# Graph convolution with experts: two dense chunks become gathered parts, and the counting one-hots are made in batches

## The chip, the cores and the metric

The kernel runs on one core of a Trainium2 chip. The metric is the device time of one execution in microseconds (us). A core has a matrix engine (TensorE, PE in the profile; PEld is its loading of the stationary operand), a vector engine (VectorE, DVE), a scalar engine (ScalarE, ACT), a general engine (GpSimd, POOL), a synchronisation engine (SyncE, SP) and sixteen DMA engines behind queues. A queue is named by the engine that issues to it, and "POOLq" or "ACTq" in a row is that engine's issuing of a transfer.

## The reference

The input is a matrix `x` of 6250 nodes by 256 features, and 200,000 edges (`src`, `dst`), sorted by `dst`. The destinations are drawn as a square of a uniform number, so that low node numbers have many edges and high ones few. The core of what is computed:

```python
deg_out = clip(segment_sum(ones, src, n), 1.0)
deg_in = clip(segment_sum(ones, dst, n), 1.0)
h = feats * rsqrt(deg_out)[:, None]
m = segment_sum(h[src], dst, n) * rsqrt(deg_in)[:, None]
xx = m @ W_gc + b_gc + feats @ W_res + b_res
core = moe_ff(xx, ...)        # top 2 of 64 experts, 256 -> 512 -> 256, gelu
y = xx + core
y = batch_norm(y) * gamma + beta
out = layernorm(feats + y)
```

The line that matters here is `m`: for every node, the sum of the rows `h[src]` over the edges that end in it.

## The kernel before

The nodes stand in 50 tiles (`NT`) of 125 (`TP`), the edges in 1563 parts of 128 (`NGU`): a part is one column of 128 lanes. The program goes through these stages; the times are those of the profiled execution.

**Degrees and projection (0 to 185 us).** For blocks of parts DVE makes one-hot matrices of the source node's tile (`hot_col`) and of its place in the tile (`hot_row`, both in the helper `hot_pairs`, L243), and TensorE multiplies them (L452), which counts the out-degrees. Between these it projects the features (`project`, L408), whose transposed tiles ACT copies (`fT`, L402). The function `split` (L153 to L342) divides each source number into tile and place; it runs for a head of 128 parts first, and for all others in the third iteration (i = 2), followed by `windows()`. In the head, ACT copies `hi_b` (L334) and `col_b` (L335), and DVE goes on from `col_b` (L340). Ahead of these ACT issues transfers of weights on its own queue (L309, L310).

**Transition (185 to 228 us).** The scale of each node is made, the projected rows `hrow` are scaled and written to `h_dram`, and DVE computes `key`, which says for each part of the dense kind and each lane the node's place in the part's window (L538 to L543); parts that don't fit are marked with a large number and go to a fallback loop after the stage, which has nothing to do for these inputs.

**Gather and dense stage (228 to 1095 us).** Two ways of summing share it. `_plan` divides the parts between them ahead of time, in the program that builds the kernel: it adds dense chunks from the first part on, as long as a modelled time of TensorE lies under a number of microseconds for each part that is left to gather.

- *Dense chunks* (the first `GD` = 1025 parts, 31 chunks, where nodes have many edges). A chunk is a run of `n` groups of `k` parts, each group covering a window of `w` nodes. For every part DVE makes a one-hot of the key against `iota_h` (`hot_of`, `hotk`, L628: 50 tiles x w columns for each lane) by a comparison with a scalar. For every eight parts it makes `lo`, the one-hot of the source's place in its tile. TensorE multiplies the two into `pc` (`count`, L638), so that `pc` counts how often each source is summed into each of the w nodes. ACT casts the counts of a group to their place in `counts` (L646); the place comes from a register that it loads from `places`. Then `multiply` (L653, L654) goes through the 50 tiles with two matmuls each, counts times `hrow`, into `sm`; ACT copies the result (`sums`, L664), and `spread` (L670, L672) puts it in its window of nodes and adds the end of the chunk before, with the one-hots `to` and `overd`. `sums_done` copies that (`resd`, L596) and SP's queue writes it to `z_dram` (L599). While chunk c is multiplied, the counts of chunk c + 1 are made.
- *Gathered parts* (the other 538, in 32 windows). POOL issues an indirect DMA that fetches the 128 rows of `h_dram` into one of six row buffers (`fetch`, L580). DVE makes a one-hot of the keys for four parts at a time (`hot`, L803), and two matmuls add the rows into the window (`pg`, L585, L586). A window that is done takes the carry of the one before (L824), is copied (`resg`, L596) and written like the others.

Beside these, finished pairs of node tiles are turned into `x` (L688 to L723), and routed to experts.

The order is written out by hand: the generator `dense()` yields pieces of work with a modelled time each, and the loop after it places one `gather(n)` whenever the modelled time passes `LEAD + n * every`, where `every` spreads the gathers evenly. In `gather`, the fetch for a buffer follows the matmuls that read it:

```python
add_rows(live["pg"], ring[n % NR], hot, g == g0, top and g == g0 + k - 1)
if n + NR < len(rows):
    fetch(ring[n % NR], srcg[:, ...])
```

**Routing (1095 to 1184 us), experts (1184 to 1655 us), norms (to the end).** Routing makes prefix counts with matmuls against triangular and all-one matrices (`upto_b`, `ones_b`). The experts' tokens are fetched and put back with indirect DMAs, and TensorE multiplies (L1273, L1285).

Of the kernel before, what the change touches and what calls it, by code (L numbers as in the profile page):

```python
# [127 lines left out]
LG = -(-GD // 32) * 32  # L134

# [10 lines left out]
def gnn_moe_kernel(ctx, tc, x_in, src, dst, bases, nexts, firsts, parts, lasts, W_gc, b_gc, W_res, b_res, Wg, bg, w1, b1, w2, b2,  # L146
# [47 lines left out]
    iota_h = const.tile([128, 512], FP16, name="iota_h")  # L194
    for k in range(4):
        V.tensor_scalar(iota_h[:, k * 128:(k + 1) * 128], iota_f, float(k * 128), None, op0=ALU.add)
# [7 lines left out]
    upto_b = const.tile([128, 128], BF16, name="upto_b")  # L204
    V.tensor_scalar(upto_b, iota_f, pidx, -1.0, op0=ALU.is_gt, op1=ALU.add)
    ones = const.tile([128, 128], F32, name="ones")
    V.memset(ones, 1.0)
    ones_b = const.tile([128, 128], BF16, name="ones_b")
    V.memset(ones_b, 1.0)
# [9 lines left out]
    with tc.tile_pool(name="edges", bufs=1) as ep, ExitStack() as later:  # L219
# [4 lines left out]
        key = ep.tile([128, GD], F32, name="key")  # L224
# [28 lines left out]
        with tc.tile_pool(name="deg", bufs=1) as dp, tc.tile_pool(name="hot", bufs=2) as hp, \  # L253
                tc.tile_pool(name="ld", bufs=2) as ld, \
                tc.tile_pool(name="ps_deg", bufs=1, space=PSUM) as ps_deg, \
                tc.tile_pool(name="ps_a", bufs=2, space=PSUM) as ps_a:
            srcf = dp.tile([128, NGR], F32, name="srcf", tag="a")
# [6 lines left out]
            G.dma_start(out=key[:, :GD], in_=bases.to_broadcast([128, GD]))  # L264
# [64 lines left out]
            def split(a, b):  # L329
# [4 lines left out]
                S.activation(hi_b[:, a:b], hi[:, a:b], AF.Copy)  # L334
                S.activation(col_b[:, a:b], hi[:, a:b], AF.Copy, scale=2.0)  # L335
# [92 lines left out]
            for i in range(NGR // CG):  # L428
# [5 lines left out]
                if i == 2:  # L434
                    split(HEAD, NGR)
                    G.tensor_tensor(following[:, :GD], following[:, :GD], key[:, :GD], ALU.subtract)
# [46 lines left out]
            fit, t1 = flags[:, 0, :], flags[:, 1, :]  # L483
            kd = dp.tile([128, GD], FP16, name="kd")
            V.tensor_tensor(kd, dstf[:, :GD], key[:, :GD], ALU.subtract)
# [57 lines left out]
            V.tensor_scalar(key[:, :GD], kd, BIG, None, op0=ALU.subtract)  # L543
# [20 lines left out]
        with tc.tile_pool(name="cnt", bufs=1) as cp, tc.tile_pool(name="rows", bufs=1) as rp, \  # L564
# [6 lines left out]
            NR = 6  # L571
# [44 lines left out]
            KB = 7  # L616
            hots, los, live = {}, {}, {}

            def hot_of(g):

                if g >= GD:
                    return
                if g % PAIRS == 0:
                    los[g // PAIRS] = hc.tile([128, PAIRS // 2, 128, 2], BF16, name="lo")
                    hot_pairs(los[g // PAIRS], lo_b, g, PAIRS, 128)
                w = DENSE[groups[g][0]][2]
                hots[g] = hc.tile([128, NT * w], BF16, name="hotk", bufs=KB, padded_shape=[128, NT * WMAX])
                V.tensor_scalar(hots[g], iota_h[:, :NT * w], key[:, g:g + 1], None, op0=ALU.is_equal)  # L628

            def count(g):  # L630
# [9 lines left out]
                hot_of(g + KB)  # L640
# [119 lines left out]
            def dense():  # L760
# [4 lines left out]

                for g in range(KB):
                    hot_of(g)
# [142 lines left out]

    b1T = ctx.enter_context(tc.tile_pool(name="b1pool", bufs=1)).tile([128, 4, E], F32, name="b1T")
# [20 lines left out]

    iota_e = rt.tile([TP, E, NT], BF16, name="iota_e")
# [587 lines left out]
```

## Time and profile before

| what | value |
| --- | --- |
| median of 3 runs | 1791.05 us (1790.22 to 1792.17) |
| profiled execution, its own time | 1785.81 us |
| its span | 1784.0 us |
| mean TensorE clock granted | 0.926 |
| TensorE busy | 1463.9 us, 82% of the span |
| VectorE busy | 991.2 us, 56% |
| ScalarE busy | 702.0 us, 39% |
| GpSimd busy | 907.8 us, 51% |

The profile is of one execution. A group's row reads: line, engine, operation, output and input names, shapes, count, then busy us and mean ns of one, then the idle time of that engine just before these instructions and what ended most of it. In a timeline row the first number is the start in us, the second the duration in us, and what stands in brackets is the idle time before it and what ended it. A window's row gives a stretch of the span, its length, the busy time of the five engines with their instruction counts, the granted TensorE clock, the DMA engines' busy share and GB/s. A row of waits has total us, times, and the longest in us.

### The profile page before, as it was taken

The numbers are of one execution on the slowest core, as the hardware profiler recorded it, in microseconds if no ns is written. First come the engines' busy times: TensorE is split into PE (matmuls) and PEld (weight loads), VectorE is DVE, ScalarE is ACT, GpSimd is POOL, SyncE is SP. The second block draws the span as 40 slices with busy tenths as digits, with TensorE's granted clock in tenths as the row PEclk, the third lists the DMA queues.
The fourth block names the chain that finished last, engine by engine and source line by source line (L and its number), as shares of the span: only waits on it lengthen the run. The fifth ranks groups of instructions, "written<-read, shape, count | busy, mean of one in ns | idle before, by whom it ended". The sixth has DMA issues, their size and how long they took to land. (4 is left out here: it accounts for less than half of the span.)

```text
span 1784.0 us, 31696 instructions
## 1 busy us (share of the span) xinstructions
PE 1463.9 (82%) x10296; PEld 1213.0 (68%) x10296; DVE 991.2 (56%) x2594; ACT 702.0 (39%) x1707; POOL 907.8 (51%) x984
## 2 busy tenths in 40 slices
PE   3999168899898899989899896369999999999730
PEld 2555047677788888888888895158878887777520
DVE  7999886666666555545454551962222222222787
ACT  2343663333455554445444441032222222222248
POOL 3241436666676666666666664025655666554000
PEclk8999678999999999999999998579999999999875
DMA  5798766776776777677776774917867888675934
GB/s 146 225 276 262 238 180 181 195 199 186 208 215 195 197 216 213 183 211 206 203 207 195 217 205 119 211 48 244 268 207 240 253 245 257 212 244 179 223 87 127
DMA packets 221104, 362.19 MB, mean 203 GB/s; under 512 B 24819, under 2 KB 149613, under 8 KB 220929
## 3 DMA queue, kind: packets, MB, share of 16 engines
q1 hardware_dynamic: 158039, 180.12, 34.7%
q0 software_dynamic: 55328, 172.48, 34.1%
q10 hardware_dynamic: 7562, 7.47, 1.5%
q8 instruction: 84, 1.38, 0.3%
q14 instruction: 91, 0.75, 0.1%
HBM read 279.11 MB, written 74.47 MB: 198 GB/s over the span
## 5 line engine op out<-in xcount | busy, mean ns | idle before, releaser
L580 POOL DMA_INDIRECT r<-h_dram,srcg x538 | 554.7, 1031 | 303.5 <-issue 109.9
L653 PE MATMUL sm<-hrow,counts 125*128 125x258 f32 x1550 | 502.2, 340 | 7.9 <-ACT counts L646 5.4
L646 ACT CAST counts<-pc 128x300 f32 (+7 forms) x804 | 355.9, 443 | 335.4 <-PE pc L638 147.0
L628 DVE TENSOR_SCALAR hotk<-iota_h,key 128x300 bf16<-128x300 f16 (+7 forms) x1025 | 272.5, 305 | 326.1 <-PE pc L638 159.4
L654 PE MATMUL sm<-hrow,counts 125*128 125x256 f32 x1550 | 417.6, 284 | 0.7 <-issue 0.7
L653 PEld LDWEIGHTS sm<-hrow,counts 125*128 125x128 f32 x1550 | 304.4, 196 | 68.8 <-issue 57.0
L638 PE MATMUL pc<-hotk,lo 128*128 128x300 bf16 (+7 forms) x1025 | 282.1, 303 | 82.3 <-issue 35.5
L654 PEld LDWEIGHTS sm<-hrow,counts 125*128 125x128 f32 x1550 | 301.2, 194 | 2.1 <-issue 1.5
L1275 ACT ACTIVATE hT<-ph,b1c 128x128 f32<-128x128 f32 (+8 forms) x256 | 108.6, 437 | 352.0 <-PE ph L1273 219.0
L1285 PE MATMUL py<-w2s,hT 128*128 128x256 f32 (+3 forms) x992 | 240.5, 385 | 3.4 <-issue 1.9
L1273 PE MATMUL ph<-xgT,w1s 128*128 128x128 f32 (+8 forms) x1024 | 211.3, 349 | 8.9 <-issue 5.4
L1273 PEld LDWEIGHTS ph<-xgT,w1s 128*128 128x128 f32 x1024 | 170.5, 192 | 42.7 <-issue 19.7
L1285 PEld LDWEIGHTS py<-w2s,hT 128*128 128x128 f32 (+3 forms) x992 | 166.4, 176 | 44.7 <-issue 6.6
L585 PE MATMUL pg<-r,hot 128*128 128x258 f32 x538 | 178.5, 332 | 19.5 <-issue 11.1
L1239 POOL DMA_INDIRECT y_dram<-ys,dest x124 | 119.1, 961 | 146.4 <-DVE ys L1288 83.5
L1239 POOL DMA_INDIRECT xg<-x_dram,ids x124 | 119.1, 960 | 111.2 <-DVE ids L1191 71.3
L586 PE MATMUL pg<-r,hot 128*128 128x256 f32 x538 | 153.3, 285 | 0.0
L1288 DVE TENSOR_TENSOR ys<-py,b2s 128x256 f32<-128x256 f32 (+3 forms) x124 | 51.3, 420 | 166.9 <-PE py L1285 117.7
L638 PEld LDWEIGHTS <-lo 128*128 128x128 bf16 x1025 | 90.0, 102 | 73.7 <-issue 23.0
L1263 DVE COPY xgT<-pte 128x256 f32<-128x256 f32 (+7 forms) x64 | 38.5, 601 | 182.2 <-PE pte L1261 71.8
L585 PEld LDWEIGHTS pg<-r,hot 128*128 128x128 f32 x538 | 104.8, 195 | 38.9 <-issue 25.0
L586 PEld LDWEIGHTS pg<-r,hot 128*128 128x128 f32 x538 | 104.7, 195 | 0.9
(321 smaller groups left out, 1775.1 us busy)
## 6 DMA issues: line engine op xcount, KB each, us to landing
w1s<-in_L_gnn_w_dram SPq DMA_DIRECT2D x64, 512.0 KB
w2s<-in_L_gnn_w_dram SPq DMA_DIRECT2D x64, 512.0 KB
y_dram<-zeros SPq DMA_DIRECT2D x48, 256.0 KB
yr<-y_dram SPq DMA_DIRECT2D x25, 448.0 KB
r<-h_dram,srcg POOLq DMA_INDIRECT x538
b2s<-in_L_gnn_b_dram SPq DMA_DIRECT2D x64, 128.0 KB
h_dram<-hrow SPq DMA_DIRECT2D x5, 1344.0 KB
z_dram<-zeros ACTq DMA_DIRECT2D x7, 903.0 KB
```

What stands on the lines that cost most here:

```text
L580: G.indirect_dma_start(out=f32(r[:, :2 * D]), out_offset=None, in_=h_dram[:, :], in_offset=bass.IndirectOffsetOnAxis(ap=idx, axis=0))
L585: T.matmul(pg, hot, r[:, D:], start=first, stop=False)
L586: T.matmul(pg[:, :D], hot, r[:, :D], start=False, stop=last)
L628: V.tensor_scalar(hots[g], iota_h[:, :NT * w], key[:, g:g + 1], None, op0=ALU.is_equal)
L638: T.matmul(pc, los[g // PAIRS][:, r // 2, :, r % 2], hots.pop(g), start=(i == 0), stop=(i == k - 1))
L646: S.copy(counts[c % 2][:, :, ds(live["at"][j % 8], w)], pc.rearrange("p (t w) -> p t w", w=w))
L653: T.matmul(sm, by, hrow[:, t, D:], start=(t == 0), stop=False)
L654: T.matmul(sm[:, :D], by, hrow[:, t, :D], start=False, stop=(t == NT - 1))
L1239: w = G.indirect_dma_start(**kw)
L1273: T.matmul(ph[:, :m], w1s[:, kk, c * 128:(c + 1) * 128], xgT[:, kk, :m], start=(kk == 0), stop=(kk == 1))
L1275: S.activation(hT[:, c, :m], ph[:, :m], AF.Gelu, bias=b1_e[:, c:c + 1])
L1285: T.matmul(py[:n], hT[:, c, k * 128:k * 128 + n], w2s[:, c, :], start=(c == 0), stop=(c == 3))
```

## The change

1. The number of microseconds that the plan sets against each gathered part goes from 1.29 to 1.2. Two chunks fewer are dense: 29 chunks with 988 parts in place of 31 with 1025. The other 29 are as before; the widest of their windows is 8 and no longer 9. Gathered are 575 parts in 34 windows in place of 538 in 32. Since the modelled work is less and the gathers more, `every` falls from 1.117 to 0.981 modelled us.
2. The fetches have eight row buffers and no longer six, so that the order holds eight fetches ahead of the first gathered matmul.
3. `resd` and `resg` have one buffer each and no longer two.
4. The one-hots `hotk` are made in batches: one comparison of two tensors for several parts at once (36 columns a tile, so 18 parts for a window of 2, 12 for 3, 8 for 4, 6 for 5 and 6, 4 for 7 and 8), laid out in pairs of parts. There are 189 of these in place of 1025 comparisons with a scalar. Two batches are held in place of seven parts. The `lo` of a block of eight parts is made one block ahead (`lo_of`).
5. The comparison needs `key` as fp16; it is computed in place of `kd`, and the windows' bases have a tile of their own, `base`.
6. In the head of `split`, DVE makes `col_b` and no longer ACT, and ACT makes `hi_b` after it.
7. The constants `ones`, `ones_b` and `upto_b` are made in the pools that use them (degrees, experts, routing), and not at the start for the whole program.

```diff
-    while 16.0 + 1.03 * (pe + (NGU - g) * 0.265) < (NGU - g) * 1.29:
+    while 16.0 + 1.03 * (pe + (NGU - g) * 0.265) < (NGU - g) * 1.2:
...
+LANES = 36
...
-        key = ep.tile([128, GD], F32, name="key")
+        key = ep.tile([128, GD + GD % 2], FP16, name="key")
...
+        cuts, cut_of = [], {}
+        for c, (g0, k, w, n) in enumerate(DENSE):
+            a = g0
+            while a < g0 + k * n:
+                b = min(a - a % 2 + LANES // w // 2 * 2, g0 + k * n)
+                for g in range(a, b):
+                    cut_of[g] = len(cuts)
+                cuts.append((a, b, w))
+                a = b
...
-                S.activation(hi_b[:, a:b], hi[:, a:b], AF.Copy)
-                S.activation(col_b[:, a:b], hi[:, a:b], AF.Copy, scale=2.0)
+                if b > HEAD:
+                    S.activation(hi_b[:, a:b], hi[:, a:b], AF.Copy)
+                    S.activation(col_b[:, a:b], hi[:, a:b], AF.Copy, scale=2.0)
+                else:
+                    V.tensor_scalar(col_b[:, a:b], hi[:, a:b], 2.0, None, op0=ALU.mult)
+                    S.activation(hi_b[:, a:b], hi[:, a:b], AF.Copy)
...
-            V.tensor_scalar(key[:, :GD], kd, BIG, None, op0=ALU.subtract)
+            V.tensor_scalar(kd, kd, BIG, None, op0=ALU.subtract)
...
-            NR = 6
+            NR = 8
...
-                res = rsp.tile([WIN, D + 2], F32, name="resd" if c < ND else "resg", bufs=2)
+                res = rsp.tile([WIN, D + 2], F32, name="resd" if c < ND else "resg")
...
-            KB = 7
+            KB = 2
...
-            def hot_of(g):
-
-                if g >= GD:
+            def lo_of(q):
+
+                if q * PAIRS < GD:
+                    los[q] = hc.tile([128, PAIRS // 2, 128, 2], BF16, name="lo")
+                    hot_pairs(los[q], lo_b, q * PAIRS, PAIRS, 128)
+
+            def hot_of(q):
+
+                if q >= len(cuts):
                     return
-                if g % PAIRS == 0:
-                    los[g // PAIRS] = hc.tile([128, PAIRS // 2, 128, 2], BF16, name="lo")
-                    hot_pairs(los[g // PAIRS], lo_b, g, PAIRS, 128)
-                w = DENSE[groups[g][0]][2]
-                hots[g] = hc.tile([128, NT * w], BF16, name="hotk", bufs=KB, padded_shape=[128, NT * WMAX])
-                V.tensor_scalar(hots[g], iota_h[:, :NT * w], key[:, g:g + 1], None, op0=ALU.is_equal)
+                a, b, w = cuts[q]
+                e, m = a - a % 2, NT * w
+                n = b + b % 2 - e
+                hot = hc.tile([128, n * m], BF16, name="hotk", bufs=KB, padded_shape=[128, NT * LANES])
+                hot = hot.rearrange("p (c j r) -> p c j r", j=m, r=2)
+                V.tensor_tensor(hot, pairs(key, e, n, m), iota_h[:, None, :m, :].to_broadcast([128, n // 2, m, 2]),
+                                ALU.is_equal)
+                for g in range(a, b):
+                    hots[g] = hot[:, (g - e) // 2, :, (g - e) % 2]
...
-                hot_of(g + KB)
+                if g % PAIRS == 1:
+                    lo_of(g // PAIRS + 1)
+                if g == cuts[cut_of[g]][1] - 1:
+                    hot_of(cut_of[g] + KB)
```

More of the change, by code (lines that the diff above doesn't have):

```diff
@@ L193, in gnn_moe_kernel @@
            allow_small_or_imprecise_dtypes=True)
-    iota_h = const.tile([128, 512], FP16, name="iota_h")
-    for k in range(4):
-        V.tensor_scalar(iota_h[:, k * 128:(k + 1) * 128], iota_f, float(k * 128), None, op0=ALU.add)
+    iota_h = const.tile([128, NT * WMAX, 2], FP16, name="iota_h")
+    for a in range(0, NT * WMAX, 128):
+        b = min(a + 128, NT * WMAX)
+        V.tensor_scalar(iota_h[:, a:b, :], iota_f[:, :b - a, None].to_broadcast([128, b - a, 2]), float(a), None,
+                        op0=ALU.add)
     iota_2 = const.tile([128, 128, 2], BF16, name="iota_2")
@@ L256, in gnn_moe_kernel @@
                 tc.tile_pool(name="ps_a", bufs=2, space=PSUM) as ps_a:
+            ones = dp.tile([128, NC], F32, name="ones")
+            V.memset(ones, 1.0)
+            ones_b = dp.tile([128, 1], BF16, name="ones_b")
+            V.memset(ones_b, 1.0)
             srcf = dp.tile([128, NGR], F32, name="srcf", tag="a")
@@ L263, in gnn_moe_kernel @@
             G.dma_start(out=first, in_=firsts.to_broadcast([128, NC]))
-            G.dma_start(out=key[:, :GD], in_=bases.to_broadcast([128, GD]))
+            base = dp.tile([128, GD], F32, name="base")
+            G.dma_start(out=base, in_=bases.to_broadcast([128, GD]))
+            V.memset(key[:, GD - 1:], 0.0)
             part = dp.tile([128, 2, ND], F32, name="part")
@@ L764, in of_one_hots @@
                     return n * k * (0.23 + 0.034 * w)
-                for g in range(KB):
-                    hot_of(g)
+                lo_of(0)
+                for q in range(KB):
+                    hot_of(q)
                 g, n = 0, DENSE[0][1] * DENSE[0][3]
@@ L909, in gnn_moe_kernel @@
             left_over = (made["below"], made["above"])
+    ones = ctx.enter_context(tc.tile_pool(name="onepool", bufs=1)).tile([128, 128], F32, name="ones")
+    V.memset(ones, 1.0)
     b1T = ctx.enter_context(tc.tile_pool(name="b1pool", bufs=1)).tile([128, 4, E], F32, name="b1T")
@@ L931, in gnn_moe_kernel @@
     rt = rtp.__enter__()
+    ones_b = rt.tile([128, 128], BF16, name="ones_b")
+    G.memset(ones_b, 1.0)
+    upto_b = rt.tile([128, 128], BF16, name="upto_b")
+    V.tensor_scalar(upto_b, iota_f, pidx, -1.0, op0=ALU.is_gt, op1=ALU.add)
     iota_e = rt.tile([TP, E, NT], BF16, name="iota_e")
```

13 lines of the change are left out of this document (3 added, 10 removed).

## The prediction

> **What bounds the kernel now.** I read the totals first, then the costliest groups, then busy time by windows, then the fetch tile and the waits of TensorE.
>
> ```profile
> PE 1463.9 (82%) x10296; PEld 1213.0 (68%) x10296; DVE 991.2 (56%) x2594; ACT 702.0 (39%) x1707; POOL 907.8 (51%) x984
> L580 POOL DMA_INDIRECT r<-h_dram,srcg x538 | 554.7, 1031 | 303.5 <-issue 109.9
> L628 DVE TENSOR_SCALAR hotk<-iota_h,key 128x300 bf16<-128x300 f16 (+7 forms) x1025 | 272.5, 305 | 326.1 <-PE pc L638 159.4
> 225.00:300.00 75.00, 55.79 (x385) 45.50 (x386) 58.23 (x235) 39.60 (x106) 34.74 (x33) 0.78 0.61 177
> 300.00:400.00 100.00, 85.73 (x603) 73.35 (x601) 64.85 (x227) 36.04 (x93) 67.22 (x66) 0.93 0.70 195
> 500.00:600.00 100.00, 89.94 (x698) 82.53 (x696) 61.12 (x214) 55.15 (x136) 67.23 (x65) 1.00 0.72 204
> 700.00:800.00 100.00, 90.06 (x666) 83.16 (x666) 55.31 (x176) 49.15 (x109) 66.07 (x65) 0.98 0.71 202
> ```
>
> In the windows the columns are length, then PE, PEld, DVE, ACT and POOL. The change lies mainly in the gather and dense stage, which runs from about 228 to 1095 us. There TensorE is busy 86 to 90% and sets the pace; POOL, which issues the 538 fetches, is busy two thirds. Only in the first 75 us is DVE the busiest engine (58.23 of 75). So the stage is balanced between TensorE (dense chunks) and POOL (gathers), and the change shifts work from the first to the second.
>
> **Moving work from dense to gathered.** What TensorE gives back goes by the spacing at which its matmuls start.
>
> ```profile
> 700.85 0.28 PE L653 MATMUL sm<-hrow,counts 125*128 125x258 f32 x1
> 700.97 0.28 PE L654 MATMUL sm<-hrow,counts 125*128 125x256 f32 x1
> 701.09 0.28 PE L585 MATMUL pg<-r,hot 128*128 128x258 f32 x1
> 249.99 0.24 PE L638 MATMUL pc<-hotk,lo 128*128 128x150 bf16 x1
> L638 PE MATMUL pc<-hotk,lo 128*128 128x450 bf16 x37 | 13.8, 372 | 0.0
> L670 PE MATMUL sm<-sums,to 128*128 128x258 f32 x61 | 18.5, 382 | 0.5 <-ACT sums L664 0.5
> ```
>
> The large matmuls start 0.12 us apart. Two chunks fewer are 200 of them: 24.0 us. 37 count matmuls fewer, at some 0.2 us (their duration is 0.372, and they overlap as the others do), are 7.4 us; the spreads of two chunks some 1.8 us. 37 gathered parts more are 74 matmuls, 8.9 us, and two windows more 0.9 us. TensorE's work falls by 23.4 us. Were it still the bound, the stage would shorten by that much. ACT casts 37 counts fewer and DVE loses a little with them; neither is the bound.
>
> What POOL takes on goes by the fetch.
>
> ```profile
> L580 POOL DMA_INDIRECT r<-h_dram,srcg x538: 942/948/1748, 245.9 to 1082.0; - x180
> L585 PE MATMUL pg<-r,hot x538: 276/287/726, 258.8 to 1085.9; 128*128 128x258 f32 x180
> 1074.29 0.95 POOL L580 DMA_INDIRECT r<-h_dram,srcg  x1 [0.30 <-issue]
> 1075.54 0.95 POOL L580 DMA_INDIRECT r<-h_dram,srcg  x1 [0.30 <-PE pg L586]
> ```
>
> A ring of six buffers means that 532 fetches start after the first gathered matmul (258.8) and the last at 1082.0: one each 823.2/532 = 1.547 us. The fetch itself takes 0.948 us at the median and 1.031 in the mean, and 0.305 us pass between two: POOL could go at 1.336 today. With eight buffers 567 fetches follow the first gathered matmul; the same end needs 823.2/567 = 1.452 us each. At 1.336 the stage would be TensorE's, whose own sum allows (823.2 - 23.4)/567 = 1.411.
>
> **Batched one-hots.** 1025 one-hots by comparison with a scalar (mean 0.305 us, 272.5 us) become 189 comparisons of two tensors, over 287,100 elements a lane. Their price I take from the same kind of operation at two sizes.
>
> ```profile
> L243 DVE TENSOR_TENSOR lo<-lo_b,iota 128x1024 bf16<-128x1024 bf16 x129 | 88.0, 682 | 0.0
> L243 DVE TENSOR_TENSOR hot_row<-row_b,iota 128x2048 bf16<-128x2048 bf16 x49 | 59.9, 1223 | 3.2 <-PE degp L452 0.5
> L803 DVE TENSOR_TENSOR hot<-keyg,iota_f 128x512 fp32r<-128x512 f16 x122 | 83.1, 682 | 9.8 <-PE pg L586 4.2 <-PE sm L654 2.2 <-PE pc L638 1.6
> ```
>
> The step from 1024 to 2048 elements costs 0.541 us, so 0.53 ns an element and 0.14 fixed: 152 + 27 = 179 us, mean 0.95 us. If the layout runs at half that rate, as the 512-element comparison with a float operand does (0.682), they would be some 330 us; bf16 out of fp16 in is nearer to the first. DVE gains 93 us, but most beside TensorE's work. On the path it counts where DVE bounds: the 114 one-hots of chunk 0.
>
> ```profile
> L628 DVE TENSOR_SCALAR hotk<-iota_h,key 128x150 bf16<-128x150 f16 x114 | 23.3, 268 | 9.3 <-PE pc L638 6.3 <-remote 2.3
> ```
>
> Ten batches of twelve parts (1800 elements, 1.1 us) replace 114 x 0.268 = 31 us by 11 us, but the chunk also has 14 lo tiles and the hots, and TensorE's 114 count matmuls, and the gathers are spread through it. Before the first gathered matmul I count -2 us (0 to -5); the rest goes into the pace.
>
> **What the batches do to the fetches.** This is the term I weigh most. In the trace a fetch is longer when a tensor_tensor of DVE runs as it begins.
>
> ```profile
> 1072.47 0.69 DVE L803 TENSOR_TENSOR hot<-keyg,iota_f 128x512 fp32r<-128x512 f16 x1 [2.72 <-PE pg L586]
> 1072.55 1.43 POOL L580 DMA_INDIRECT r<-h_dram,srcg  x1 [0.30 <-PE pg L586]
> 251.01 1.01 DVE L628 TENSOR_SCALAR hotk<-iota_h,key 128x150 bf16<-128x150 f16 x4 [0.43 <-PE pc L638]
> 251.46 0.97 POOL L580 DMA_INDIRECT r<-h_dram,srcg  x1 [0.30 <-issue]
> ```
>
> The fetch at 1072.55 began under a comparison that ended at 1073.16, and took 0.48 more than the median: 1073.16 - 1072.55 - 0.13. The one at 251.46 began among the scalar comparisons and took 0.97. So a tensor_tensor of length d, met at an even chance, costs the fetches (d - 0.13)²/2. Now: 251 (lo and hot) of 0.682 are 251 x 0.152 = 38 us, spread over some 850 us 0.045 a fetch; measured are 1.031 - 0.948 = 0.083, 1.84 times it. After: 254 x 0.152 + 189 x 0.336 = 102 us, over 830 us 0.123 a fetch, so 0.078 more. The period is 1.336 + 0.078 = 1.414, or with the factor 1.84 1.336 + 0.144 = 1.480. I take 1.44, between them and above TensorE's 1.411. End of the fetches: 258.8 + 567 x 1.44 = 1075.3 against 1082.0: -6.7 us. With waits of 0.04 on top of the higher period, 1.52: +39; at 1.37, -46.
>
> The Trainium skill, "SBUF — State Buffer", section "Who interferes with whom", says it the other way round: a scalar comparison in a two-port mode holds the port pair that GpSimd shares, while a tensor_tensor with two SBUF inputs contends only with GpSimd work that reads SBUF, and, as an inference there, not with descriptor writing. By it the batches would relieve the fetches and the period would fall to about 1.25 (estimate by that page); the two rows above disagree with it, and the measurement decides.
>
> **The ring of eight and single result buffers.** TensorE's waits from 300 to 1080:
>
> ```profile
> PE pc L638 <- issue: 34.2, 58, 1.4
> PE pc L638 <- DVE hotk L628: 8.0, 8, 1.9
> PE pc L638 <- ACT counts L646: 6.5, 8, 1.4
> PE pg L585 <- DMA r<-h_dram,srcg: 4.3, 7, 1.3
> ```
>
> Two more buffers can take at most the 4.3 us of fetched rows; counted in the pace. With one buffer for resd and for resg, the copy (L596) waits until the matmul that reads the last one is over. The copy's own input, the running window, ends after that matmul, so I cost it at 0 (up to 30 x 0.4 if a signal is late). Two batches ahead in place of seven parts: a batch waits for the last count of the one two before, and the counts behind it then for DVE; today's 8.0 us bound it from below, double that from above. I take no change.
>
> **The start.** Here the change moves one small operation.
>
> ```profile
> 13.66 0.27 ACTq L310 DMA_DIRECT2D bgate<-in_L_gnn_bg_dram  x1
> 14.20 0.29 ACT L335 ACTIVATE col_b<-hi 128x128 bf16<-128x128 f32 x1
> 14.52 0.29 DVE L340 SCALAR_TENSOR_TENSOR col_b<-row_b,col_b 128x128 bf16<-128x128 bf16 x1 [7.36 <-ACT col_b L335]
> 26.45 0.90 DVE L153 TENSOR_SCALAR hi<-srcf 128x1440 f32<-128x1440 f32 x1
> 41.79 1.54 PE L452 MATMUL degp<-hot_col,hot_row 128*64 128x100 bf16 x32 [12.15 <-DVE hot_col L243]
> 4.81 0.23 DVE L153 TENSOR_SCALAR hi<-srcf 128x128 f32<-128x128 f32 x1
> ```
>
> DVE idles 7.36 us for a column that ACT makes only after its queue has issued its transfers. From there DVE runs on to the large split (26.45) and the one-hots for which TensorE waits 12.15 us at 41.79; after it TensorE bounds the loop to 181. In the changed kernel DVE makes the column itself (0.23 us, as the row of that size). The chain moves up 7.36 - 0.3 = 7 us, and since TensorE's wait (12.15) is longer, so does the loop: -7 us. If ACT's other work of these tiles (fT, the projection) is late instead, 3 remain.
>
> **The keys, the constants.** The key is finished in place as fp16.
>
> ```profile
> 220.91 1.10 DVE L543 TENSOR_SCALAR key<-kd 128x1025 f32<-128x1025 f16 x1
> 216.61 0.43 DVE L540 TENSOR_SCALAR kd<-kd 128x1025 f16<-128x1025 f16 x1
> ```
>
> 1.10 becomes 0.43, and the others shrink by 37/1025: -1 us on the chain that ends in the first one-hot. The constants made at routing are a memset and one comparison of 128 x 128, up to 0.3 us each, beside the wait for the last sums: 0. DMAs: two writes of sums by chunk less, two by window more on SP's queue, fetches of 37 parts more on POOL's own. Share of the DMA engines 0.70 to 0.72 in the windows; not the bound.
>
> **Sum.** -7 - 1 - 2 - 6.7 = -16.7 us. The profiled execution took 1785.81 us (1784.0 of span, 1.8 around it), which gives 1769; the median shown is 1791.05, 5.2 above it, and 1791.05 - 16.7 = **1774 us**.
>
> **Rivals.**
> 1. *The stage stays TensorE's, and its waits shrink too* (my term for the fetches is too large). For it: POOL is idle a third of the time today, with 303.5 us before its fetches. Against: the row at 1072.55. At TensorE's 1.411 less the 8.0 and 4.3 us of waits, 1.39: stage -35, in all -45: 1746. The rule of the Trainium skill cited above ("SBUF — State Buffer", "Who interferes with whom") would lead here too.
> 2. *The fetches are the bound and slower than I say; the kernel is slower than before.* One mechanism: the batches hold the fetches longer than (d - 0.13)²/2 on average, for DVE and POOL are coupled (a batch is released by counts that follow a gather). From 1.452 + 10/567 = 1.47 us a fetch on, the gains ahead of it (10 us) are eaten. At the 1.84-fold lengthening and 0.03 of waits, 1.51: +33 - 10 = +23, 1814. For it: the factor of 1.84 that the trace shows and I cannot place. Against: six buffers already absorb single long fetches, and eight absorb more.
> 3. *The start's gain does not arrive* (TensorE bound by projections): the sum is -12.7, 1778. It is within the range of my own forecast.
>
> **How the numbers follow.** My forecast, 1763 to 1785 by periods from 1.42 to 1.46 (5.67 us for each 0.01): 0.42. Rival 1: 0.25. Rival 2: 0.25. Near zero, the gap between: 0.08. Of runs of this kernel, less than 0.2% (3.6 us) cannot be told from none. Faster: 0.42 + 0.25 = 0.67; within 0.2%: 0.08; slower: 0.25. The range reaches from 1740 (rival 1) to 1808 (rival 2 by most of its width).
>
> **What would show it.** Right: the fetches' mean rises from 1031 ns to 1110 or more while the median stays near 948; they start each 1.44 us; POOL is busy over 75% in the windows from 400 on and TensorE below 88%; the batches are near 0.95 us each; the wait of 7.36 us at 14.52 is gone and the projection loop ends 7 us sooner. Wrong: a fetch mean near 1.03 (rival 1), a period above 1.47 (rival 2), or batches at twice the price, which would bring DVE near 80% of the first chunks and TensorE's waits for hotk well above 8.0 us.

## The result and the profile after

The changed kernel takes 1831.94 us (median; 1825.89 to 1839.5) against 1791.08 us of the kernel before on the same chip: 1.0247 times as long, with a 95% interval of 1.0217 to 1.0276. It is 41 us slower; forecast were 17 us less, and the range ended at 1808. On two other groups of runs, told below, the ratio was 1.0269 [1.0239, 1.0299] and 1.0317 [1.0277, 1.0357].

Totals and costliest groups of the changed kernel's profile, then windows (length, then PE, PEld, DVE, ACT, POOL), then the fetch and its first matmul, then TensorE's waits from 300 to 1110 us:

```profile
PE 1475.1 (80%) x10127; PEld 1230.3 (67%) x10127; DVE 929.1 (51%) x1764; ACT 679.1 (37%) x1664; POOL 976.3 (53%) x1022
L596 POOL DMA_INDIRECT r<-h_dram,srcg x575 | 627.6, 1092 | 282.9 <-issue 122.1
L650 DVE TENSOR_TENSOR hotk<-key,iota_h 128x1400 bf16<-128x1400 f16 (+6 forms) x189 | 179.2, 951 | 288.0 <-PE pc L663 90.6
```

```profile
300.00:400.00 100.00, 83.66 (x555) 73.19 (x555) 49.94 (x77) 34.03 (x89) 72.52 (x67) 0.85 0.68 195
500.00:600.00 100.00, 88.00 (x644) 80.63 (x642) 49.53 (x104) 50.38 (x128) 71.33 (x65) 0.93 0.73 210
700.00:800.00 100.00, 84.75 (x594) 78.72 (x594) 45.11 (x94) 43.31 (x102) 69.92 (x64) 0.90 0.68 192
```

```profile
L596 POOL DMA_INDIRECT r<-h_dram,srcg x575: 947/953/2954, 241.7 to 1131.2; - x192
L601 PE MATMUL pg<-r,hot x575: 276/288/777, 255.6 to 1140.8; 128*128 128x258 f32 x192
```

```profile
PE pc L663 <- issue: 54.0, 47, 3.5
PE pc L663 <- ACT counts L674: 17.3, 17, 4.0
PE pc L663 <- DVE hotk L650: 9.5, 6, 4.6
PE pg L601 <- DVE hot L832: 9.2, 4, 5.3
```

The fetches start each (1131.2 - 255.6) / 567 = 1.544 us. Before, it was 1.547. So the 35 fetches more that follow the first gathered matmul (567 against 532) took their full 1.54 us, as if the two dense chunks had cost nothing. The window rows say the same in another way: in each 100 us POOL issues as many fetches as before (64 to 67), while TensorE does fewer matmuls (594 against 666 from 700 to 800). TensorE is less busy, POOL is busy 70 to 73%, and neither is full (what full looks like for each is measured below: 100% for TensorE, 77% for POOL).

The whole loss is in the gather and dense stage. The last fetch starts 49.2 us later than before (1131.2 against 1082.0), and the span is 49.6 us longer (1833.6 against 1784.0). These are single executions, which took 1835.44 and 1785.81 us; the medians differ by 41.

The start gained less than forecast. The rows are of DVE, and the last one of TensorE:

```profile
6.58 0.57 DVE L351 TENSOR_SCALAR col_b<-hi 128x128 bf16<-128x128 f32 x1
16.43 0.90 DVE L154 TENSOR_SCALAR hi<-srcf 128x1440 f32<-128x1440 f32 x1
28.00 1.66 DVE L357 SCALAR_TENSOR_TENSOR col_b<-row_b,col_b 128x1440 bf16<-128x1440 bf16 x1 [6.91 <-ACT col_b L349]
38.69 1.55 PE L469 MATMUL degp<-hot_col,hot_row 128*64 128x100 bf16 x32 [10.73 <-DVE hot_col L250]
```

DVE no longer waits for the head's column and begins the large split 10 us sooner (16.43 in place of 26.45). DVE's own column takes 0.57 us, where 0.23 were forecast. But the large split has a column too, which ACT still makes, behind a copy of a projection: DVE waits 6.91 us for it at 28.00. TensorE goes on at 38.69, 3.1 us sooner than before, and the first gathered matmul is 3.2 us sooner (255.6 against 258.8), where the terms ahead of it were forecast at 10.

### The profile page after: what moved, and what is told of

Read it like the earlier page. It is cut to its first block, busy times and chain, and to the rows that moved or that the text cites. A ratio compares the mean times of both kernels' runs of the same rounds, so it can differ in the third digit from the quotient of the medians.

```text
span 1833.6 us, 30593 instructions
## 1 busy us (share of the span) xinstructions
PE 1475.1 (80%) x10127; PEld 1230.3 (67%) x10127; DVE 929.1 (51%) x1764; ACT 679.1 (37%) x1664; POOL 976.3 (53%) x1022
## 5 line engine op out<-in xcount | busy, mean ns | idle before, releaser
L596 POOL DMA_INDIRECT r<-h_dram,srcg x575 | 627.6, 1092 | 282.9 <-issue 122.1
L681 PE MATMUL sm<-hrow,counts 125*128 125x258 f32 x1450 | 488.1, 350 | 7.0 <-ACT counts L674 5.0
L674 ACT CAST counts<-pc 128x300 f32 (+6 forms) x767 | 334.8, 436 | 380.3 <-PE pc L663 148.8
L663 PE MATMUL pc<-hotk,lo 128*128 128x300 bf16 (+6 forms) x988 | 278.5, 316 | 115.1 <-issue 58.1
L681 PEld LDWEIGHTS sm<-hrow,counts 125*128 125x128 f32 x1450 | 299.2, 206 | 58.1 <-issue 48.2
L650 DVE TENSOR_TENSOR hotk<-key,iota_h 128x1400 bf16<-128x1400 f16 (+6 forms) x189 | 179.2, 951 | 288.0 <-PE pc L663 90.6
L682 PEld LDWEIGHTS sm<-hrow,counts 125*128 125x128 f32 x1450 | 294.8, 203 | 4.8 <-issue 4.1
L601 PE MATMUL pg<-r,hot 128*128 128x258 f32 x575 | 199.5, 347 | 22.8 <-DVE hot L832 9.2
L602 PE MATMUL pg<-r,hot 128*128 128x256 f32 x575 | 169.5, 295 | 1.9 <-issue 1.9
L601 PEld LDWEIGHTS pg<-r,hot 128*128 128x128 f32 x575 | 118.3, 206 | 52.9 <-issue 35.7
L832 DVE TENSOR_TENSOR hot<-keyg,iota_f 128x512 fp32r<-128x512 f16 (+3 forms) x156 | 100.6, 647 | 68.0 <-PE pc L663 31.7
```

The lines of the kernel that those rows point to most:

```text
L596: G.indirect_dma_start(out=f32(r[:, :2 * D]), out_offset=None, in_=h_dram[:, :], in_offset=bass.IndirectOffsetOnAxis(ap=idx, axis=0))
L601: T.matmul(pg, hot, r[:, D:], start=first, stop=False)
L602: T.matmul(pg[:, :D], hot, r[:, :D], start=False, stop=last)
L650: V.tensor_tensor(hot, pairs(key, e, n, m), iota_h[:, None, :m, :].to_broadcast([128, n // 2, m, 2]), ALU.is_equal)
L663: T.matmul(pc, los[g // PAIRS][:, r // 2, :, r % 2], hots.pop(g), start=(i == 0), stop=(i == k - 1))
L674: S.copy(counts[c % 2][:, :, ds(live["at"][j % 8], w)], pc.rearrange("p (t w) -> p t w", w=w))
```

## The experiments

Each group of runs shares one chip and its own runs of the kernel before. That kernel's time differs much between the groups: 1768, 1667, 1786, 1668 and 1667 us. This turned out to matter. "The pace" below is the time from the first gathered matmul to the start of the last fetch, divided by the number of fetches less the number of buffers; where half of the fetches are left out, it is the time from the first gathered matmul to the last, divided by 574.

### Which part costs the time

The theory after the first reading: a gathered part costs its 1.54 us whatever the rest does. The rivals: the batches cost it, by lengthening the fetches, or the ring of eight does.

a_plan: the kernel before with the new division alone.

```diff
-    while 16.0 + 1.03 * (pe + (NGU - g) * 0.265) < (NGU - g) * 1.29:
+    while 16.0 + 1.03 * (pe + (NGU - g) * 0.265) < (NGU - g) * 1.2:
```

> The kernel before with the new division alone: 29 dense chunks, 575 gathered parts, everything else (six buffers, one-hots by part, two result buffers, the start) as before. If a gathered part costs its 1.54 us whatever the rest of the kernel does (the changed kernel still gathers at (1131.2 - 255.6) / 567 = 1.544 us), the 37 parts more cost 37 x 1.547 = 57 us and this run is near 1845 us. If the batched one-hots are what made the changed kernel slow, this run keeps TensorE's saving: 1765 to 1785 us.

b_oldplan: the changed kernel with 1.29 again in that line.

> The changed kernel with the old division alone (31 dense chunks, 538 gathered parts). If the division costs the time: near 1785 us, the start's few us below the kernel before. If the batches or the ring cost it: 1820 us or more.

c_nr6: the changed kernel with six buffers.

```diff
-            NR = 8
+            NR = 6
```

> The changed kernel with six row buffers. If the ring of eight lets fetches crowd and makes TensorE's signals later: 1795 to 1810 us. If the ring does not matter: 1832 us within 5. If it helps, 1840 us or more.

d_perpart: the changed kernel with one-hots by part, f32 keys and `KB = 7`. Of its diff only the main line stands here; the rest puts back the tiles and the calls of the kernel before.

```diff
-                V.tensor_tensor(hot, pairs(key, e, n, m), iota_h[:, None, :m, :].to_broadcast([128, n // 2, m, 2]),
-                                ALU.is_equal)
+                V.tensor_scalar(hots[g], iota_h[:, :NT * w], key[:, g:g + 1], None, op0=ALU.is_equal)
```

> The changed kernel with one-hots by part, compared with a scalar (f32 keys as before, seven of them ahead), all else as changed. If the batches lengthen the fetches (1092 ns in the mean against 1031) and that is the cost: 1775 to 1790 us, with a fetch mean back near 1035 ns. If the division is the cost: within 10 of 1832 us, though the fetch mean falls.

The kernel before took 1767.68 us here.

| run | time, us | ratio [95%] | gathered parts | pace, us |
| --- | --- | --- | --- | --- |
| a_plan | 1815.51 | 1.029 [1.0246, 1.0333] | 575 | 1.511 |
| b_oldplan | 1761.09 | 0.9957 [0.9935, 0.9978] | 538 | 1.538 |
| c_nr6 | 1805.84 | 1.0221 [1.0181, 1.0261] | 575 | 1.514 |
| d_perpart | 1810.0 | 1.0261 [1.0212, 1.0311] | 575 | 1.513 |

The division alone costs 48 us, which is 1.29 us for each of the 37 parts and a little less than the 57 expected; all the rest of the change together gains 6.6. The fetch and its first matmul in a_plan, b_oldplan and d_perpart, in this order:

```profile
L580 POOL DMA_INDIRECT r<-h_dram,srcg x575: 951/957/1904, 245.0 to 1118.1; - x192
L585 PE MATMUL pg<-r,hot x575: 278/292/777, 258.5 to 1124.3; 128*128 128x258 f32 x192
```

```profile
L596 POOL DMA_INDIRECT r<-h_dram,srcg x538: 943/950/2450, 239.1 to 1064.3; - x180
L601 PE MATMUL pg<-r,hot x538: 277/286/777, 249.4 to 1073.6; 128*128 128x258 f32 x180
```

```profile
L593 POOL DMA_INDIRECT r<-h_dram,srcg x575: 947/954/1993, 238.7 to 1110.5; - x192
L598 PE MATMUL pg<-r,hot x575: 278/286/717, 252.6 to 1119.5; 128*128 128x258 f32 x192
```

The groups of the fetches in c_nr6 and d_perpart, which differ in batches and one-hots by part (and by the ring):

```profile
L596 POOL DMA_INDIRECT r<-h_dram,srcg x575 | 625.1, 1087 | 267.9 <-issue 117.4 <-PE pc L663 61.7 <-PE pg L602 46.6
```

```profile
L593 POOL DMA_INDIRECT r<-h_dram,srcg x575 | 585.5, 1018 | 307.4 <-issue 129.3 <-PE pc L654 70.0 <-PE sm L672 45.4
```

Without the batches a fetch takes 1018 ns and no longer 1087, as forecast. The pace does not move at all. What the fetch itself saves, POOL waits (307.4 us before the fetches in place of 267.9). So the lengthening is real and costs nothing in this group. For the ring, a_plan (six buffers) and d_perpart (eight), both with one-hots by part, have paces of 1.511 and 1.513. The changed kernel itself, with eight, was not run in this group. The 1805.84 us of c_nr6 lie where a harmful ring was expected (1795 to 1810), but these bounds were made for a group in which the kernel before took 23 us more; its ratio of 1.0221 and the 1.0247 of eight buffers have intervals that overlap.

### Fetches, bytes or matmuls

e_plan15: the changed kernel with the division moved the other way, 1.5 in that line: 34 dense chunks, 485 gathered parts.

> The changed kernel with the division moved the other way: 1.5 for each gathered part, 34 dense chunks and 485 gathered parts. If the fetches set the pace (1.51 us each in all four runs so far, whichever the division), 53 parts fewer than in the kernel before are 53 x 1.5 = 80 us less, about 1690 us, unless TensorE takes over. If TensorE bounds the kernel before, three chunks more (16.5 us each, less 53 x 0.24) are 37 us more: about 1800 us. Between these: both are close to binding.

f_halffetch:

```diff
-                if n + NR < len(rows):
+                if n + NR < len(rows) and n // NR % 2 == 0:
```

> The changed kernel with every second round of the ring not fetched (the matmuls read what the buffers hold, so half of the gathered sums are of wrong rows); all matmuls, one-hots and copies stay. If fetches set the pace, the stage falls to TensorE's own sum, by 75 us or more: below 1735 us. If the gathered matmuls, the copies or the order of the work set it: within 15 us of 1806, which the same kernel with six buffers took.

g_halfrows (one hunk of two; the other sets the unfetched halves of the buffers to zero):

```diff
-                G.indirect_dma_start(out=f32(r[:, :2 * D]), out_offset=None, in_=h_dram[:, :],
+                G.indirect_dma_start(out=f32(r[:, :D]), out_offset=None, in_=h_dram[:, :].rearrange("n (k d) -> (n k) d", k=2),
```

> The changed kernel with fetches of rows half as long (1 KB, the first half of the right bytes' number but of other rows; sums wrong), as many fetches as before. If the bytes that land in SBUF are the cost: between 1806 and the run with half of the fetches. If it is the issuing of a fetch on POOL: within 10 us of 1806.

h_onematmul:

```diff
-                T.matmul(pg, hot, r[:, D:], start=first, stop=False)
-                T.matmul(pg[:, :D], hot, r[:, :D], start=False, stop=last)
+                T.matmul(pg, hot, r[:, D:], start=first, stop=last)
```

> The changed kernel with one of the two matmuls of each gathered part left out (half of the sum is missing): 575 matmuls of 0.12 us fewer on TensorE. If TensorE's own work bounds the stage: 69 us less, about 1737 us. If the fetches set the pace: within 10 us of 1806.

Here the kernel before took 1666.5 us, 100 less than in the group above, and e_plan15 1678.54: a ratio of 1.0068 [1.0046, 1.009], neither the gain of 80 us nor the loss of 37 that were expected. The other three run into the fallback path after the stage (12.6 ms in all), so only the stage is read from them. Since the kernel before was faster here too, the expectations' 1806 does not serve as a measure; the runs compare with each other, and with l_after below, which is the changed kernel under the same condition at a pace of 1.377.

The first row is e_plan15's window from 500 to 600, the next its fetch; then f_halffetch's window from 700 to 800 and its gathered matmul, and the fetches of g_halfrows and h_onematmul:

```profile
500.00:600.00 100.00, 100.00 (x790) 93.49 (x789) 57.51 (x116) 62.67 (x149) 69.14 (x64) 1.00 0.74 207
L596 POOL DMA_INDIRECT r<-h_dram,srcg x485: 942/949/2454, 241.1 to 984.1; - x162
```

```profile
700.00:800.00 100.00, 100.00 (x774) 95.12 (x773) 58.22 (x129) 54.33 (x118) 43.34 (x40) 1.00 0.53 149
L601 PE MATMUL pg<-r,hot x575: 277/286/562, 250.5 to 934.8; 128*128 128x258 f32 x192
```

```profile
L597 POOL DMA_INDIRECT r<-h_dram,srcg x575: 949/954/1852, 242.8 to 1034.4; - x192
```

```profile
L596 POOL DMA_INDIRECT r<-h_dram,srcg x575: 949/954/1842, 240.9 to 1034.3; - x192
```

With half of the fetches and all matmuls, 575 gathered parts take (934.8 - 250.5) / 574 = 1.19 us each. TensorE is busy for 679.5 of these 684 us, so this is its own sum; I had put it at 800. With all fetches the pace is 1.381 with half the bytes and 1.384 with half of the gathered matmuls, against 1.377 with neither edit. In e_plan15 TensorE is busy 100.00 of 100 us, with 790 matmuls: that is what TensorE at its limit looks like. The kernel before, which I read as TensorE's bound at 89.94, had 698 there, 0.88 of that.

### The same in a group where the kernel before is slow

i_before and i_after are the two kernels unchanged, so that all traces come from one chip; i_halfrows and i_halffetch are the edits of g and f.

> The kernel before, unchanged, so that its trace and the others of this group come from one chip (chips differ: this kernel took 1791, 1768 and 1666 us on three of them). Ratio 1.00. If the chip is one where it takes near 1666 us, the fetches should start every 1.34 to 1.36 us and ScalarE should see TensorE's counts 0.1 us after their end; if near 1770 to 1790, every 1.54 us and 2 us late.

> The changed kernel, unchanged, on the same chip. On a chip with prompt signals the fetches run back to back at 1.092 + 0.305 = 1.40 us: 567 x 1.40 = 794 against 532 x 1.35 = 718, so 60 to 75 us slower (ratio near 1.04). On a chip with late signals: 40 to 50 us slower (1.025), as measured on two. If the theory that TensorE's sum decides held anywhere, it would be 20 us faster.

> The changed kernel with fetches of 1 KB rows (wrong rows; only the time of the gather and dense stage is read, not the total, since what follows runs through another path on such sums). On a chip with prompt signals the period is 1.38 us, as once measured. On a chip with late signals: if the landing bytes delay TensorE's signals, the period falls from 1.51-1.54 to about 1.38 and the delay goes; if the number of fetches does, the period stays above 1.48.

> The changed kernel with every second round of the ring not fetched (sums of wrong rows; only the stage is read). If fetches alone set the pace, the stage's 575 gathered parts take 1.19 us each on any chip, and the signals are prompt (0.1 us) wherever half of the fetches are gone. If the chip's signals are late by themselves: above 1.4 us a part with signals still 1 us late or more.

The kernel before took 1786.29 us (i_before 1787.6), i_after 1830.29: 1.0269 [1.0239, 1.0299]. Fetch and first matmul of i_before, i_after and i_halfrows, and the matmul of i_halffetch:

```profile
L580 POOL DMA_INDIRECT r<-h_dram,srcg x538: 942/947/1685, 244.1 to 1083.0; - x180
L585 PE MATMUL pg<-r,hot x538: 278/287/781, 258.6 to 1088.3; 128*128 128x258 f32 x180
```

```profile
L596 POOL DMA_INDIRECT r<-h_dram,srcg x575: 947/954/3177, 243.0 to 1128.3; - x192
L601 PE MATMUL pg<-r,hot x575: 277/287/781, 253.5 to 1136.9; 128*128 128x258 f32 x192
```

```profile
L597 POOL DMA_INDIRECT r<-h_dram,srcg x575: 947/954/2454, 243.9 to 1126.5; - x192
```

```profile
L601 PE MATMUL pg<-r,hot x575: 278/286/528, 254.6 to 952.1; 128*128 128x258 f32 x192
```

The paces are 1.550 (i_before), 1.543 (i_after) and 1.540 (i_halfrows, whose first gathered matmul starts at 253.5 too). Half the bytes change nothing here either. With half of the fetches a gathered part takes (952.1 - 254.6) / 574 = 1.215 us, and TensorE is busy for 683.4 of the 697.5. So in both kinds of group it is the fetches, and not their bytes, that hold the changed kernel's stage above TensorE's sum.

What differs between the kinds is how soon the other engines go on after a matmul's end. The windows from 500 to 700 of i_after and i_halffetch, and then a count and its cast in i_after and in l_after:

```profile
500.00:700.00 200.00, 178.26 (x1255) 164.50 (x1255) 97.27 (x210) 95.66 (x234) 141.29 (x129) 0.91 0.73 205
```

```profile
500.00:700.00 200.00, 196.66 (x1523) 184.40 (x1522) 116.57 (x247) 113.75 (x267) 89.42 (x80) 0.99 0.52 146
```

```profile
697.16 0.31 PE L663 MATMUL pc<-hotk,lo 128*128 128x300 bf16 x1
701.52 0.41 ACT L674 CAST counts<-pc 128x300 f32 x1 [1.06 <-PE pg L602]
```

```profile
704.66 0.33 PE L663 MATMUL pc<-hotk,lo 128*128 128x350 bf16 x1
705.09 0.99 ACT L674 CAST counts<-pc 128x350 f32 x2 [1.72 <-PE pc L663]
```

In i_after ScalarE has been idle for 1.06 us when it casts, at 701.52, a count that ended at 697.47: 4.05 us late (casts follow the counts in program order; this pair is the same group in the program). In l_after the cast starts 0.10 us after the count's end. The delay is not a fixed one: the four casts from 697.14 to 701.52 start some 1.47 us apart while their counts ended 0.63 us apart, so that it grows from 1.56 to 4.05.

Over all casts of a trace before which ScalarE stood idle (by more than 0.15 us), each paired with the last count of its group, the delay at the median is:

| run | casts | delay, us | delayed over 0.5 us |
| --- | --- | --- | --- |
| before | 404 | 2.19 | 85% |
| after | 415 | 1.62 | 72% |
| i_before | 380 | 2.13 | 85% |
| i_after | 425 | 1.40 | 67% |
| i_halffetch | 419 | 0.09 | 32% |
| l_after | 478 | 0.09 | 4% |

With half of the fetches most casts of the late group are prompt, but not all, which is less than was expected. The releaser in the row is a sign of a late start: the cast does not depend on the gathered matmul L602, which merely ended last. POOL starts late too, where it waits at all: in i_after 82 of the 567 fetches begin more than 0.45 us after the fetch before them has ended, and these begin 4.15 us (median) after the matmul that frees their buffer; in e_plan15 it is 143 of 477, and 0.27 us. (Over all fetches the delay tells nothing: in l_after, where POOL is never idle, it is 5.10.)

What the traces show is late starts. Whether the signal of a matmul's end comes late, or the waiting engine is slow to go on for a reason of its own, no run here separates; "late signals" and "prompt signals" are names for the two kinds of group.

### The other side, rows, and the change under prompt signals

j_plan15 is e_plan15 again. j_plan14 has 1.4 in the line of the division: 33 dense chunks, 502 gathered parts. j_rows64 fetches into 64 lanes (a second hunk sets the buffers to zero):

```diff
-                G.indirect_dma_start(out=f32(r[:, :2 * D]), out_offset=None, in_=h_dram[:, :],
-                                     in_offset=bass.IndirectOffsetOnAxis(ap=idx, axis=0))
+                G.indirect_dma_start(out=f32(r[:64, :2 * D]), out_offset=None, in_=h_dram[:, :],
+                                     in_offset=bass.IndirectOffsetOnAxis(ap=idx[:64], axis=0))
```

> 34 dense chunks and 485 gathered parts in the changed kernel, once more, in case this chip is one on which TensorE's signals come late. There, if each fetch costs 1.54 us of the stage until TensorE's own sum binds, 53 fetches fewer than in the kernel before are up to 82 us less, but TensorE's sum of this division, which took 734 us on a chip with prompt signals, keeps it from falling under 823 - 734 = 89 us: about 1710 to 1735 us where the kernel before takes 1770 to 1790. On a chip with prompt signals: 1.007 times the kernel before, as measured.

> 33 dense chunks and 502 gathered parts in the changed kernel. If fetches bind (late signals): 36 fewer than before, 36 x 1.54 = 55 us less, about 1730 us where the kernel before takes 1786. If TensorE binds (prompt signals): 16 us x 2 more less 36 x 0.24 = 23 us on top of its sum, within 10 us of the kernel before.

> The changed kernel with fetches of 64 rows in place of 128, as many fetches (half of each gathered part's rows are not fetched; only the stage is read). Halving the bytes of each row left the pace at 1.540 us. If the number of rows, so of descriptors, sets what a fetch costs, the pace falls towards TensorE's 1.2 us and the signals become prompt; if it is the fetch instruction itself, the pace stays above 1.48 us on a chip with late signals.

l_after is the changed kernel; l_plan14 and l_rows64 repeat j_plan14 and j_rows64, to see them under late signals.

> The changed kernel unchanged, beside the next two. Where TensorE's signals come late (the kernel before at 1765 to 1790 us): ratio 1.025 as before. Where they are prompt (the kernel before at 1667): the fetches run back to back at 1.39 us, 567 x 1.39 = 788 us in place of some 720, so 1730 to 1740 us, ratio 1.04. TensorE's sum binding would give 1650.

> 33 dense chunks and 502 gathered parts in the changed kernel. Prompt signals: 1.005 times the kernel before, as measured, with TensorE busy all through the stage. Late signals: if each fetch costs 1.54 us, 36 fewer are 55 us less, a ratio of 0.97; if the late signals hold up TensorE's own work instead, above 1.0.

> The changed kernel with fetches of 64 rows (only the stage is read). Prompt signals: back to back at 1.36 us, as once measured (1.041 + 0.305). Late signals: if the rows of a fetch are what makes the signals late, well under 1.5 us; if the fetch itself does, above 1.48.

Both groups came out with prompt signals (the kernel before at 1667.67 and 1666.89 us). j_plan15 took 1676.89, 1.0049 [1.0033, 1.0066]; j_plan14 1676.15, 1.0047 [1.0028, 1.0066]; l_plan14 1679.78, 1.0066 [1.0043, 1.0088]; l_after 1718.52, 1.0317 [1.0277, 1.0357]. Fetches of l_after (tile and group) and its window from 500 to 600, then the fetches of j_rows64:

```profile
L596 POOL DMA_INDIRECT r<-h_dram,srcg x575: 949/954/1830, 241.5 to 1031.2; - x192
L596 POOL DMA_INDIRECT r<-h_dram,srcg x575 | 615.1, 1070 | 196.8 <-issue 78.8 <-PE pc L663 51.0 <-PE pg L602 29.6
500.00:600.00 100.00, 93.06 (x712) 85.49 (x712) 56.35 (x120) 55.37 (x134) 77.26 (x72) 0.98 0.81 231
```

```profile
L597 POOL DMA_INDIRECT r<-h_dram,srcg x575: 907/912/2395, 241.2 to 1013.8; - x192
```

In l_after the first gathered matmul starts at 250.4, so the pace is (1031.2 - 250.4) / 567 = 1.377, and the fetch's mean and the gap are 1.070 + 0.305 = 1.375: POOL fetches back to back through the whole stage, and in the window this reads as 77% busy, since the gaps of 0.305 count as idle; TensorE, at 93%, is not the bound. 37 parts more at 1.377 are 51 us, and the whole change cost 51.6; but the kernel before was traced in no group with prompt signals, so that it too ran at the fetches' pace there is not shown. With 64 rows the pace is (1013.8 - 250.5) / 567 = 1.346 (first matmul at 250.5; l_rows64 has 1013.2), still back to back: a fetch costs nearly the same for half the rows (912 ns against 954 at the median). With 485 or 502 gathered parts nothing is gained under prompt signals, since TensorE then binds (100.00 of 100 us from 500 to 600 in e_plan15).

What stays open: why the engines go on late in some groups while fetches run and not in others (the same chip number stood in a late and in a prompt group), whether the rows of a fetch matter in a late group, and whether fewer gathered parts pay there. No run of 33 or 34 chunks fell into a late group.

## Why the prediction was wrong

**The step that failed** is the first: "There TensorE is busy 86 to 90% and sets the pace". From it came TensorE's sum of 823 - 23.4 = 800 us, which is 680 to 683 by the half-fetch runs, and the reading of POOL's idle third as room. In the terms of the working, the period before was POOL's possible 1.336 us and 0.211 of waiting. The working took the 0.211 for TensorE's work, dropped it whole, and added 0.10 for longer fetches: 1.44. Measured are 1.092 + 0.305 for the fetch and its gap, and 0.147 of waiting: 1.544. So the lengthening was somewhat less than forecast (0.061), and the waiting, which was put at nothing, stayed. That it was not TensorE's work, the half-fetch runs show: with all matmuls and half of the fetches the stage falls to 684 and 697 us. In l_after the waiting is gone (1.377 against 1.375); there the fetches set the pace by themselves, and the change still costs 52 us.

So a part moved to the gathers cost most of its period: 48 us for 37 in a_plan, where 37 x 1.511 = 56. The two chunks that were dropped gave back some 8 us, and not the 33 of the working (24.0 + 7.4 + 1.8), since TensorE's own work was not what the stage waited for. The arithmetic at the end holds: its point of balance was 1.47 us a fetch, and (1.544 x 567) - 823 = +52, less the start's 3, is the +49 of the two profiled executions.

**Where the trace could have shown it.** The busy share said it as it stood: at 90% a tenth of the stage is idle. From the first gathered matmul to the last, TensorE was busy 743.2 of 827.3 us in the kernel before. With 743 in place of 823 the working's own sum allows (743.2 - 23.4) / 567 = 1.27 us, under POOL's 1.336, and the question would have been what POOL waits for. The mean length of a matmul does not tell it. The same group in the kernel before and in e_plan15, where TensorE is full:

```profile
L653 PE MATMUL sm<-hrow,counts 125*128 125x258 f32 x1550 | 502.2, 340 | 7.9 <-ACT counts L646 5.4
L681 PE MATMUL sm<-hrow,counts 125*128 125x258 f32 x1700 | 543.6, 337 | 3.2 <-DMA h_dram<-hrow 3.2
```

ScalarE's waits tell more (total, times, longest): three rows of the kernel before from 300 to 1080 us, and three of l_after from 300 to 1000:

```profile
ACT counts L646 <- PE pc L638: 127.3, 164, 2.4
ACT counts L646 <- PE pg L586: 72.8, 80, 3.8
ACT counts L646 <- PE sm L654: 55.5, 53, 3.3
```

```profile
ACT counts L674 <- PE pc L663: 225.6, 395, 3.5
ACT counts L674 <- PE pg L602: 5.0, 15, 0.4
ACT counts L674 <- PE sm L682: 3.9, 4, 2.3
```

Half of the casts' waits in the kernel before, 72.8 + 55.5 of 255.6 us, are put down to matmuls on which a cast does not depend: the count it needs had ended before. In l_after it is 8.9 of 234.5.

**Batches.** Right in size: 189 of 951 ns, 179.2 us, forecast 0.95 and 179. The working set them against 31 us of one-hots in chunk 0, where its own row has 23.3 us busy: these overlap, and their number times their mean is too much.

**The lengthening of fetches.** Right in its mechanism, too large, and without effect on the pace where signals are late. Forecast were 1110 ns or more; measured were 1092, 1097 and 1070. In i_before the mean is 1178 ns for fetches that begin while a tensor_tensor of DVE alone runs (79 of them), 988 where it is a comparison or other operation with a scalar (197), and 953 where it is neither (224). The Trainium skill, "SBUF — State Buffer", section "Who interferes with whom", has it the other way round for the writing of descriptors, as an inference; these rows disagree with it. Under prompt signals the lengthening does count, since POOL then runs back to back.

**The rivals.** Rival 1 (TensorE stays the bound) was wrong by the half-fetch runs. Rival 2 had the side and the sign that would show it (a period above 1.47), and 1814 was nearer than 1774; its mechanism, a further lengthening by the batches, was not it: d_perpart is as slow without batches. Rival 3 had the start's size right (3 us of the 7 remain). The head's wait was won, and the same kind of wait took 6.91 us back one step later, at the large split's column, which ScalarE makes only after a copy that waits for TensorE's projection.

**The ring and the single result buffers.** Costed at nothing, and no run contradicts it: with six buffers the pace is 1.514, as with eight in d_perpart (1.513). The single buffers were not tried alone. The granted clock fell from 0.926 to 0.903. It is not the cause: a_plan has 0.929 at a ratio of 1.029, and l_after 0.932 at the largest.

The version that beats both kernels, by 0.4%, is b_oldplan, the change without its new division: 0.9957 [0.9935, 0.9978], in a group with late signals; it was not run under prompt ones.

## What to carry to other kernels

When work can be moved between two engines that are both below full, find out what the stage costs with half of one kind left out, before taking either for the bound. Learn what full looks like for each: here TensorE reads 100% when it is the bound, and POOL 77%. A busy share of 90% says that a tenth is idle, and the wall time of a stage is not the work of its busiest engine. A gathered part more cost 1.29 us here (a_plan), with fetches 1.35 to 1.55 us apart that half the bytes made no cheaper; by these runs, moving work there can pay only as long as TensorE's own sum lies above the number of fetches times their period.

## What was not expected of the hardware

A fetch of 128 rows costs POOL 954 ns at the median with rows of 2 KB and of 1 KB alike, and 912 ns with 64 rows. In some groups of runs, and not in others, ScalarE goes on 1.4 to 2.2 us (median) after a count's end while POOL issues a fetch every 1.54 us. With half of the fetches the median there is 0.09 us, though 32% of the casts still start over 0.5 us late. The same program takes 1786 us in one group and 1667 in another.
